# Self attention and FFN of a perceiver layer: lists of steps with distances in place of alternating generators

## The chip, the cores and the metric

The kernel runs on one core of a Trainium2 chip, in float32 with bfloat16 in the feed-forward part. The metric is the device time of the whole program in microseconds, the median of repeated runs.

## The reference

One perceiver layer on 64 batch rows. `x` has 64 rows of 64 tokens of 256 features, the context 64 rows of 256 tokens. Three sublayers follow each other, each with a residual:

```python
x = x + xattn(layernorm(x), ctx, ctx)   # 16 heads of 16; 64 queries on 256 keys of the same batch row
x = x + attn(layernorm(x))              # causal self attention, 16 heads of 16, 64 tokens
x = x + ffn(layernorm(x))               # gate, up: 256 -> 1024; down: 1024 -> 256

def _act_quant(x):                      # each row of activations to 8-bit whole numbers
    scale = 127.0 / clip(max(abs(x), axis=-1), 1e-05)
    return clip(round(x * scale), -128, 127) / scale
# weights: to -1, 0, 1 times the mean of their absolute values
gate = silu(bitlinear(x, w_gate)); up = bitlinear(x, w_up)
return bitlinear(gate * up, w_down)
```

## The kernel before

**Tiling.** The 64 batch rows form 8 groups of 8 (G = 8). A group has 512 tokens, 4 tiles of 128 (NI = 4). `x` of a group is one tile of 128 x 4 x 256 with 4 buffers (`load_x`, L79). The context comes for two batch rows at a time (`load_ctx`, L84, 2 buffers). PSUM holds one tile of four banks for cross attention's scores (`ps_sc`, L66) and four tiles of one bank for everything else (`mm_tile`, L69). A new `mm_tile` waits until the last reader of the tile that had its bank is done.

**The order of the work** is written out by hand: from L630 on, the program order of each engine (TensorE, ScalarE, VectorE, GpSimd) is the order in which the Python code issues. An engine works through its queue in that order.

**The main loop** (L644) has one iteration for each batch row n; I call it a *place*, and count the places 1 to 8 of a group of eight (n % 8 = 0 is place 1). A place does cross attention for its row:

- `max_rows` (L271): TensorE transposes the row maxima (`mtp`, L273), ScalarE copies them (`mT`, L275);
- `probabilities` (L278): scores transposed (`scT`, L286 and L293), exp on ScalarE (`PT`, L299), sums of two halves on GpSimd (`PS`, L301);
- `project` (L617): a quarter of the keys or values of the next pair of rows, twice (`k_a`, L209; `v_a`, L229), copied by ScalarE (L222, L232);
- `scores_max` (L250) for the next row: scores (`sc`, L258), their maxima on VectorE (`nm`, L262), and four small VectorE operations that split them into three bfloat16 parts (L265 to L268), which the next `mtp` reads;
- `cross_av` (L305): products with the values and sums (`av`, L313, L318), and ScalarE's `keep` (L322). The rest, `cross_out` (L325: three VectorE operations that read `av` and write `yT_a`), is done in the next place, after `mtp` is issued.

**Filler work.** While group g does cross attention, the self attention of group g-1 and the FFN of group g-2 are done in between. `prepare` (L594) normalises the next group's x and makes its queries, one `yield` in each place. Self attention (`self_attention`, L332) and FFN (`ffn`, L482) are Python generators. `fill` (L578) is called six times in each place (48 times in a group): it takes one step, up to the next `yield`, from one of the two generators, in turn. Self attention has 24 steps, the FFN 19, so both are through before a group ends; `drain` (L586) takes what is left at the start of the next group.

What a step gives to VectorE is in the step itself, with two exceptions, which go into a list `later` and are issued at the start of the next `fill`: the product of `silu` and `up` (`hidden`, L522) and `keep` of self attention (L420).

Steps of self attention that matter here: `add_projected` (L234: two tiles of output projection `o_a` or `o_s` for one VectorE add of 128 x 512 at L242), `ln_stats` (L167), `ln_rstd` (L173, seven GpSimd operations), `ln_apply` (L187), `transposed` (`tp_s`), queries and keys, `scores` (`ssc`, L366; VectorE adds the mask and takes maxima, L372, L375; GpSimd subtracts, L376), `exps` (L380), `normalise` (VectorE sums and reciprocals, L386, L387; GpSimd multiplies, L388), `transpose` (`stp`, L396, copied at L401), `product` (`sav`, L411, L417).

Of the FFN: `ln_rstd`, `ln_apply`, `row_scale` (L469) and the rounding (L495, L498), the transposes `qtp` (L504, copied at L506); then for tile i the two halves of `gate_up` (L510; `silu`, L517), `scale_hidden` (L526: absolute maxima and small operations on VectorE, then ScalarE's scaling, L529), `round_hidden` (L531), `turn_hidden` (`hqtp`, L538, copied at L540), `down` (L542) and its add (L547). The result is stored by a DMA on GpSimd's queue (L565).

**The tail** (L683 to L689). After the last row, self attention 7 and FFN 6 alternate without cross attention, then FFN 7 runs alone.

Of the kernel before, what the change touches and what calls it, by code (L numbers as in the profile page):

```python
# [55 lines left out]
def tile_perceiver(ctx: ExitStack, tc: tile.TileContext, a: dict, out: bass.AP):  # L57
# [39 lines left out]
    bqc, bqkc = constant("bq_c"), constant("bqk_c")  # L97
    sel = constant("sel", BF16)
# [28 lines left out]
    def out_bias(w, vcol, brow, name):  # L127

        rep = small.tile([P, KC, P], F32, tag="rep", name=f"rep_{name}", bufs=1)
# [57 lines left out]
    def ln_apply(src, mv, y, name):  # L187

        xn = act.tile([P, NI, D], F32, tag="xn", name=f"xn_{name}", bufs=3)
        for i in range(NI):  # L190
            nc.vector.tensor_scalar(xn[:, i, :], src[:, i, :], mv[:, i, 0:1], y[:, i:i + 1],
                                    ALU.subtract, ALU.mult)
        return xn
# [40 lines left out]
    def add_projected(w, yT, xg, name, i0):  # L234

        pm = mm_tile(f"o_{name}_{i0}")
        for i in range(2):
            for kc in range(KC):
                nc.tensor.matmul(pm[:, i * D:(i + 1) * D],  # L239
                                 yT[:, kc, (i0 + i) * P:(i0 + i + 1) * P], w[:, kc, :],  # L240
                                 start=(kc == 0), stop=(kc == KC - 1))
        nc.vector.tensor_tensor(xg[:, i0:i0 + 2, :], pm.rearrange("p (i d) -> p i d", d=D),  # L242
                                xg[:, i0:i0 + 2, :], ALU.add)
# [61 lines left out]
    def cross_av(n, pT, pS, v):  # L305
# [17 lines left out]
        return a4, t  # L323
# [7 lines left out]

    def self_attention(g, xg, yTa):  # L332
        nm = f"s{g}"
        mv = moments(nm)
        for i0 in range(0, NI, 2):
            add_projected(wT["o"], yTa, xg, f"a{g}", i0)
            ln_stats(xg, nm, mv, (i0, i0 + 1))
            yield
        y = ln_rstd(mv, nm)
        yield  # L340
        xn = ln_apply(xg, mv, y, nm)
        yield
        xnT = act.tile([P, KC, NT], F32, tag="xnT", name=f"xnT_{nm}")
        for kc in range(KC):
            transposed(xn, nm, xnT, kc)
        yield
        qm = act.tile([P, KC, G, 2, T], F32, tag="sqm", name=f"sqm_{g}", bufs=1)
        kT = act.tile([P, KC, NT], F32, tag="skT", name=f"skT_{g}", bufs=1)
        v = act.tile([P, NI, D], F32, tag="sv", name=f"sv_{g}", bufs=1)
        for hg in range(KC):  # L350
            queries(wqkv, bqm2, xnT, nm, qm, hg)
            yield
            keys(wqkv, D, bqkc[:, KC + hg:KC + hg + 1], xnT, nm, kT, hg)
            yield
        yT = act.tile([P, KC, NT], F32, tag="yT", name=f"yT_{nm}", bufs=3)
        s, pTs = {}, {}

        def scores(hg, j0):
# [3 lines left out]
            for b in range(G):  # L362
                for h in range(2):
                    for i in range(2):
                        r = slice(2 * E * (j0 + i), 2 * E * (j0 + i + 1))
                        nc.tensor.matmul(scs[i][h * T:(h + 1) * T, b * T:(b + 1) * T],  # L366
                                         qm[r, hg, b, h, :], kT[r, hg, b * T:(b + 1) * T],
                                         start=True, stop=True)
            for i in range(2):
                k = f"{nm}_{hg}_{j0 + i}"  # L370
                t = s[hg, j0 + i] = att.tile([P, G, T], F32, tag="s", name=f"s_{k}", bufs=4)
                nc.vector.tensor_tensor(t, scs[i].rearrange("p (b k) -> p b k", k=T),  # L372
                                        causal.unsqueeze(1).to_broadcast([P, G, T]), ALU.add)
                mx = small.tile([P, G], F32, tag="smax", name=f"smax_{k}")
                nc.vector.tensor_reduce(mx, t, AX.X, ALU.max)  # L375
                nc.gpsimd.tensor_tensor(t, t, mx.unsqueeze(2).to_broadcast([P, G, T]), ALU.subtract)  # L376
# [5 lines left out]
        def normalise(hg, j0):  # L382
            for j in (j0, j0 + 1):
                t = s[hg, j]
# [97 lines left out]
    def ffn(g, xg):  # L482
# [67 lines left out]
        for i in range(NI + 3):  # L550
            if i < NI:
                gate_up(i, 0)
            if 0 < i <= NI:
                scale_hidden(i - 1)
# [201 lines left out]
```

## Time and profile before

| | us |
|---|---|
| runs, median of 3 (1131.37 to 1132.72) | 1131.42 |
| the profiled execution | 1134.02 |
| its span, first to last instruction | 1132.3 |
| start, up to the first place of group 1 | 130.4 |
| group 1 (no FFN yet) | 111.4 |
| group 2 | 128.5 |
| groups 3 to 6, each | 129.6 to 129.7 |
| group 7, its first seven places | 116.2 |
| from the last place to the end | 127.1 |

The stretches are taken from the start times of `mtp`, one in each place. In the page, PE is TensorE's matmuls, PEld its weight loads, DVE VectorE, ACT ScalarE, POOL GpSimd; a float32 matmul stands there as two. PEclk is the granted clock of TensorE in tenths, in 40 slices of the span. A row of a window table gives a stretch in us from the span's start, its length, then busy us (and instructions) of PE, PEld, DVE, ACT and POOL, TensorE's granted clock, the DMA share and GB/s. A row of waits gives who waited, for whom, the us in total, how often, and the longest. A row of groups gives line, engine, operation, tiles out<-in, shapes and count, then busy us, mean ns of one, idle us before them and what ended it.

### The profile page before, as it was taken

The numbers are of one execution on the slowest core, as the hardware profiler recorded it, in microseconds if no ns is written. First come the engines' busy times: TensorE is split into PE (matmuls) and PEld (weight loads), VectorE is DVE, ScalarE is ACT, GpSimd is POOL, SyncE is SP. The second block draws the span as 40 slices with busy tenths as digits, with TensorE's granted clock in tenths as the row PEclk, the third lists the DMA queues.
The fourth block names the chain that finished last, engine by engine and source line by source line (L and its number), as shares of the span: only waits on it lengthen the run. The fifth ranks groups of instructions, "written<-read, shape, count | busy, mean of one in ns | idle before, by whom it ended". The sixth has DMA issues, their size and how long they took to land.

```text
span 1132.3 us, 28299 instructions
## 1 busy us (share of the span) xinstructions
PE 955.4 (84%) x12366; PEld 645.5 (57%) x12366; DVE 785.4 (69%) x1560; ACT 591.9 (52%) x862; POOL 405.1 (36%) x452
## 2 busy tenths in 40 slices
PE   6987888988899898998898898998989988977655
PEld 3554556665576556665575555765566655754533
DVE  2566757566787867777777867867777756877745
ACT  2423354436764377535764367644775357626624
POOL 0344436232255313542254413451336312541520
PEclk9978998999999898998989998998989988998857
DMA  6111000100001000010001000010001000000000
GB/s 219 58 57 57 20 20 3 39 20 20 20 2 58 20 20 20 21 57 20 20 2 58 20 20 20 20 58 20 2 20 39 20 20 1 3 21 1 1 19 19
DMA packets 10059, 32.65 MB, mean 29 GB/s; under 512 B 2128, under 2 KB 2640, under 8 KB 9552
## 3 DMA queue, kind: packets, MB, share of 16 engines
q1 hardware_dynamic: 7056, 26.22, 6.5%
q0 software_dynamic: 1152, 4.19, 0.9%
q8 instruction: 97, 1.59, 0.6%
q10 hardware_dynamic: 1728, 0.43, 0.2%
q14 instruction: 26, 0.21, 0.1%
HBM read 26.65 MB, written 4.19 MB: 27 GB/s over the span
## 4 chain that ended last, share of the span: by engine, by line
PE 51%; DVE 21%; ACT 10%; issue 6%; POOL 2%; POOLq 0%; ACTq 0%; DVEq 0%
PE k_a L209 6%; PE sc L258 5%; PE av L313 4%; PE v_a L229 4%; PE scT L293 4%; ACT PT L299 3%; DVE nm L262 3%; PE ssc L366 3%; PE down_f L545 3%; PE o_s L239 3%; PE q_s L209 2%; PE stp L396 2%; PE v_s L229 2%; PE q_a L209 2%; PE av L318 2%
## 5 line engine op out<-in xcount | busy, mean ns | idle before, releaser
L301 POOL TENSOR_TENSOR PS<-PT 128x512 f32<-128x512 f32 x128 | 160.3, 1273 | 363.4 <-ACT PT L299 363.4
L262 DVE TENSOR_REDUCE nm<-sc 128x8 f32<-128x2048 f32 x64 | 146.6, 2290 | 142.1 <-PE sc L258 142.1
L299 ACT ACTIVATE PT<-scT 128x1024 f32<-128x1024 f32 x128 | 124.0, 1021 | 86.4 <-PE scT L293 79.9
L209 PE MATMUL k_a<-cT,wk 128*128 128x512 f32 x256 | 125.2, 613 | 8.8 <-DMA wk<-in_wk_dram 5.5
L229 PE MATMUL v_a<-wv,cT 128*128 128x256 f32 x512 | 129.4, 397 | 2.3 <-ACT qm L217 2.2
L376 POOL TENSOR_TENSOR s_s<-s_s,smax_s 128x512 f32<-128x512 f32 x64 | 66.7, 1047 | 158.0 <-DVE smax_s L375 154.5
L229 PEld LDWEIGHTS v_a<-wv,cT 128*128 128x128 f32 x512 | 96.1, 196 | 22.3 <-issue 4.6
L322 ACT ACTIVATE keep<-av,par 128x256 f32<-128x256 f32 x64 | 30.3, 473 | 118.4 <-PE av L318 99.6
L258 PE MATMUL sc<-kT,qm 32*128 32x256 f32 x1024 | 78.7, 423 | 14.3 <-ACT PT L299 12.3
L523 DVE SCALAR_TENSOR_TENSOR h_f<-up_f,units,silu_f 128x512 f32<-128x512 f32 x64 | 47.7, 746 | 58.6 <-ACT silu_f L517 32.8
L388 POOL TENSOR_TENSOR s_s<-s_s,stot_s 128x512 f32<-128x512 f32 x64 | 68.9, 1098 | 39.3 <-ACT spT L401 30.1
L293 PE MATMUL scT<-qm,kT 32*128 32x128 f32 x2048 | 81.5, 285 | 0.0
L209 PEld LDWEIGHTS k_a<-cT,wk 128*128 128x128 f32 x256 | 47.5, 195 | 52.3 <-issue 40.6
L313 PE MATMUL av<-PT,v 128*32 128x128 f32 x2048 | 74.7, 289 | 1.7 <-ACT PT L299 1.7
L293 PEld LDWEIGHTS scT<-qm,kT 32*128 32x128 f32 x2048 | 74.7, 201 | 0.4
L258 PEld LDWEIGHTS sc<-kT,qm 32*128 32x128 f32 x1024 | 48.7, 194 | 45.5 <-ACT PT L299 25.5
L222 ACT ACTIVATE kT<-k_a,bk_c 128x512 f32<-128x512 f32 x64 | 44.3, 691 | 53.8 <-PE k_a L209 53.3
L313 PEld LDWEIGHTS av<-PT,v 128*32 128x32 f32 x2048 | 55.6, 115 | 25.5 <-issue 20.5
L372 DVE TENSOR_TENSOR s_s<-ssc,causal 128x512 f32<-128x512 f32 x64 | 43.9, 685 | 29.2 <-PE ssc L366 28.5
L327 DVE RECIPROCAL keep<-keep 128x128 f32<-128x128 f32 x64 | 61.0, 953 | 2.2
L366 PE MATMUL ssc<-skT,sqm 32*64 32x64 f32 x2048 | 45.4, 240 | 17.5 <-ACT silu_f L517 11.9
L232 ACT COPY v<-v_a 128x512 f32<-128x512 f32 x64 | 37.5, 587 | 43.1 <-PE v_a L229 43.1
(153 smaller groups left out, 1885.8 us busy)
## 6 DMA issues: line engine op xcount, KB each, us to landing
cT<-in_ctx_dram SPq DMA_DIRECT2D x32, 512.0 KB, 3.3
x<-in_x_dram SPq DMA_DIRECT2D x8, 512.0 KB, 3.5
out_dram<-x POOLq DMA_DIRECT2D x8, 512.0 KB, 3.0
wffn_gate<-in_wgate_dram SPq DMA_DIRECT2D x1, 1024.0 KB, 6.0
wffn_up<-in_wup_dram SPq DMA_DIRECT2D x1, 1024.0 KB, 5.4
wffn_down<-in_wdown_dram SPq DMA_DIRECT2D x1, 1024.0 KB, 5.4
wqkv<-in_wqkv_dram SPq DMA_DIRECT2D x1, 768.0 KB, 6.1
wk<-in_wk_dram SPq DMA_DIRECT2D x1, 256.0 KB, 4.2
```

The costliest lines, as they stand in the source:

```text
L209: nc.tensor.matmul(pm, w[:, kc, c0:c0 + P], src[:, kc, :], start=(kc == 0), stop=(kc == KC - 1))
L229: nc.tensor.matmul(pm[:, i * D:(i + 1) * D], src[:, kc, (i0 + i) * P:(i0 + i + 1) * P], w[:, kc, c0:c0 + D], start=(kc == 0), stop=(kc == ...
L258: nc.tensor.matmul(sc[:, j, hg * S:(hg + 1) * S], qm[r, hg, b, :, :].rearrange("p h q -> p (h q)"), kT[r, hg, k0:k0 + S], start=True, stop ...
L262: nc.vector.tensor_reduce(nm, sc.rearrange("p j (c s) -> p j c s", s=S), AX.X, ALU.max, negate=True)
L293: nc.tensor.matmul(sc[:, j, o:o + P], kT[r, hg, k0 + c * P:k0 + (c + 1) * P], qm[r, hg, b, :, :].rearrange("p h q -> p (h q)"), start=Fals ...
L299: nc.scalar.activation(pT[:, j:j + 2].rearrange("p j c k n -> p j (c k n)"), sc[:, j:j + 2, :], AF.Exp)
L301: nc.gpsimd.tensor_tensor(pS[:, j:j + 2], pT[:, j:j + 2, :, 0, :], pT[:, j:j + 2, :, 1, :], ALU.add)
L313: nc.tensor.matmul(av[2 * E * j:2 * E * (j + 1), hg * P:(hg + 1) * P], v[:, (n % 2) * SC + c, d0:d0 + 2 * E], pT[:, j, hg, c, :], start=(c ...
L327: nc.vector.reciprocal(t[:, KC:, :], t[:, KC:, :])
L366: nc.tensor.matmul(scs[i][h * T:(h + 1) * T, b * T:(b + 1) * T], qm[r, hg, b, h, :], kT[r, hg, b * T:(b + 1) * T], start=True, stop=True)
L376: nc.gpsimd.tensor_tensor(t, t, mx.unsqueeze(2).to_broadcast([P, G, T]), ALU.subtract)
L388: nc.gpsimd.tensor_tensor(t, t, tot.unsqueeze(2).to_broadcast([P, G, T]), ALU.mult)
```

## The change

Self attention and FFN become lists of steps. A step is a triple: whether it gives TensorE work, a distance, and a function. A step may run only when that many places of the order (calls of `fill`) have passed since the step before it. Both lists together have 40 steps with TensorE work (26 and 14), and `fill` is called five times in each place, 40 times in a group.

```diff
-    streams = [iter(()), iter(())]
+    LEFT = 4
+    streams = [[], []]
+    count = [1, 1]
+    ready = [0, 0]
+    place = [0]
     later = []
-    turn = [0]
+    owner = [None]
 
-    def flush():
-        while later:
-            later.pop(0)()
-
-    def fill(k=1):
-        for _ in range(k):
-            flush()
-            for _ in range(2):
-                turn[0] = 1 - turn[0]
-                if next(streams[turn[0]], 0) is None:
-                    break
+    def flush(us=1e9):
+        while later and us > 0:
+            t, f = later.pop(0)
+            us -= t
+            f()
+
+    def run(k):
+        if any(o == k for o in owner[1:]):
+            flush()
+            del owner[1:]
+        _, _, f = streams[k].pop(0)
+        had = len(later)
+        f()
+        if len(later) > had:
+            owner.append(k)
+        if streams[k]:
+            ready[k] = place[0] + streams[k][0][1]
+
+    def fill():
+        place[0] += 1
+        able = [k for k in range(2) if len(streams[k]) > LEFT * k and ready[k] <= place[0]]
+        for k in list(able):
+            if not streams[k][0][0]:
+                run(k)
+                if not streams[k] or ready[k] > place[0] or not streams[k][0][0]:
+                    able.remove(k)
+        if able:
+            run(max(able, key=lambda k: (not k and len(streams[0]) > count[0] - NI,
+                                         len(streams[k]) / count[k] - 0.25 * k)))
```

`LEFT = 4`: the last four steps of an FFN wait in the list until the next FFN's steps are appended (`begin`), so they run in the next group, ahead of that FFN's head. `finish(0)` takes the place of `drain` for self attention; the FFN isn't drained.

The main loop (`cross_out` is now in `later` too, put there by `cross_av`):

```diff
         mT = max_rows(n, ms)
-        if kept is not None:
-            cross_out(n - 1, *kept, yTs[(n - 1) // G])
+        flush()
         if b == 0 and g:
-            drain(0)
-            drain(1)
-            streams[:] = [self_attention(g - 1, xs[g - 1], yTs[g - 1]),
-                          ffn(g - 2, xs[g - 2]) if g > 1 else iter(())]
+            finish(0)
+            begin(0, self_attention(g - 1, xs[g - 1], yTs[g - 1]))
+            if g > 1:
+                begin(1, ffn(g - 2, xs[g - 2]))
         fill()
+        if b == 2:
+            next(ahead, None)
+        flush()
         pT, pS = probabilities(n, qms[g], kTs[bp], mT)
         fill()
+        flush()
         if bp + 1 < B // 2:
             project(bp + 1, 2 * (n % 2))
         fill()
+        flush()
         if n + 1 < B:
             ms = scores_max(n + 1, qms[(n + 1) // G], kTs[(n + 1) // 2])
-        kept = cross_av(n, pT, pS, vs[bp])
+        cross_av(n, pT, pS, vs[bp], yTs[g])
         next(ahead, None)
         fill()
         if bp + 1 < B // 2:
             project(bp + 1, 2 * (n % 2) + 1)
-        fill(2)
-        if b == 0 and g + 1 < NG:
+        fill()
+        if b == 1 and g + 1 < NG:
+            if g > 2:
+                while len(streams[1]) > count[1]:
+                    run(1)
             if g:
                 xs[g + 1] = load_x(g + 1)
             ahead = prepare(g + 1)
```

The lists of steps:

```diff
+        return [
+            *(step(True, 1, (add_cross, i)) for i in range(NI)), step(False, 1, (root,)),
+            step(False, 2, (norm,)), step(True, 1, (turn, 0)), step(True, 1, (turn, 1)),
+            step(True, 1, (query, 0)),
+            step(True, 1, (key, 0)), step(True, 1, (query, 1)), step(True, 1, (key, 1)),
+            step(True, 1, (scores, 0, 0)), step(True, 1, (value, 0)), step(True, 1, (scores, 0, 2)),
+            step(True, 1, (value, 2), (exps, 0, 0)), step(False, 1, (normalise, 0, 0), (exps, 0, 2)),
+            step(True, 2, (transpose, 0, 0), (normalise, 0, 2)), step(True, 1, (scores, 1, 0)),
+            step(True, 1, (transpose, 0, 2)), step(True, 1, (scores, 1, 2)),
+            step(True, 1, (product, 0), (exps, 1, 0)), step(False, 1, (normalise, 1, 0), (exps, 1, 2)),
+            step(True, 2, (transpose, 1, 0), (normalise, 1, 2)), step(False, 1, (add_bias, xg, bo2_r, 0)),
+            step(True, 1, (transpose, 1, 2)), step(True, 1, (product, 1), (add_bias, xg, bo2_r, 2)),
+            *(step(True, 1, (add_self, i)) for i in range(NI))]
...
+        def first_half(i):
+            if i >= 2 and i - 2 < NI:
+                round_hidden(i - 2)
+            if i < NI:
+                gate_up(i, 0)
+            if i >= 3:
+                down(i - 3)
+        def second_half(i):
+            if i < NI:
+                gate_up(i, 512)
+            if 0 < i <= NI:
+                later.append((2.1, lambda: scale_hidden(i - 1)))
+            if i >= 2:
+                turn_hidden(i - 2)
...
+        steps = [(False, 1, root), (False, 2, norm), (False, 1, row_scales), (False, 2, round_rows),
+                 (True, 1, turn_rows)]
+        for i in range(NI + 3):
+            steps.append((True, 1, lambda i=i: first_half(i)))
+            if i < NI + 2:
+                steps.append((True, 1, lambda i=i: second_half(i)))
+        return steps + [(False, 1, store)]
```

The VectorE part of most steps goes into `later`: masked scores and maxima with GpSimd's subtraction, the division, the adds of the projections with their statistics, the FFN's row scales and rounding products, the `silu` product, `scale_hidden`, the subtraction of `round_hidden`, the add of `down`. ScalarE's scaling of the hidden rows moves from `scale_hidden` to `round_hidden`, a step later.

Smaller edits: `add_projected` does one tile of 256 columns instead of two; the line that loads the constants `bq_c` and `bqk_c` stands twice; `rep` takes a buffer of the tag `PS` instead of its own; `xn` has 2 buffers instead of 3; `prepare` issues its statistics in one step, through `later`, and its queries a `yield` later; x of the next group is loaded in place 2 instead of 1, after what is left of the FFN before has run.

The tail:

```diff
-    drain(0)
-    drain(1)
-    streams[:] = [self_attention(NG - 1, xs[NG - 1], yTs[NG - 1]), ffn(NG - 2, xs[NG - 2])]
-    fill(60)
-    streams[:] = [ffn(NG - 1, xs[NG - 1]), iter(())]
-    fill(60)
+    finish(0)
+    begin(0, self_attention(NG - 1, xs[NG - 1], yTs[NG - 1]))
+    begin(1, ffn(NG - 2, xs[NG - 2]))
+    while streams[0]:
+        fill()
+        flush()
+    begin(1, ffn(NG - 1, xs[NG - 1]))
+    finish(1)
```

## The prediction

> **What bounds the kernel now.** I read the page's busy shares and slices first, then the busy times of each engine in the eight places (places 1 to 8: one batch row each, from one transpose of the row maxima, L273, to the next) of one steady group, then TensorE's waits in that group, then the rows by form, and last the two stretches after the last place.
>
> ```profile
> PE 955.4 (84%) x12366; PEld 645.5 (57%) x12366; DVE 785.4 (69%) x1560; ACT 591.9 (52%) x862; POOL 405.1 (36%) x452
> PEclk9978998999999898998989998998989988998857
> ```
>
> TensorE is the busiest, but 84% is a mean over unlike stretches, and the clock row has dents. One group, place by place (columns: length, busy times, granted clock):
>
> ```profile
> 629.60:641.50 11.90, 11.15 (x131) 7.72 (x130) 8.93 (x21) 3.85 (x6) 2.49 (x2) 1.00 0.13 45
> 641.50:660.70 19.20, 14.75 (x147) 10.37 (x146) 12.85 (x31) 8.38 (x12) 4.59 (x8) 0.82 0.09 28
> 660.70:677.00 16.30, 15.73 (x138) 7.90 (x138) 11.41 (x25) 12.75 (x17) 4.54 (x8) 1.00 0.01 2
> 677.00:698.20 21.20, 16.67 (x287) 12.66 (x286) 14.47 (x31) 17.21 (x21) 4.49 (x4) 0.96 0.08 26
> 698.20:716.30 18.10, 17.75 (x232) 11.94 (x231) 15.33 (x31) 11.69 (x17) 9.08 (x8) 0.86 0.00 1
> 716.30:731.30 15.00, 14.20 (x281) 10.67 (x277) 11.90 (x18) 8.21 (x13) 7.29 (x7) 1.00 0.01 4
> 731.30:749.60 18.30, 15.65 (x219) 10.00 (x214) 12.93 (x20) 9.93 (x18) 11.42 (x11) 1.00 0.24 88
> 749.60:759.30 9.70, 9.56 (x131) 7.42 (x129) 8.17 (x19) 3.21 (x5) 4.58 (x8) 1.00 0.01 2
> sum 129.70, PE 115.46 PEld 78.68 DVE 96.00 ACT 75.24 POOL 48.49; mean PE 14.43 PEld 9.84 DVE 12.00 ACT 9.40 POOL 6.06
> ```
>
> A group takes 129.7 us: TensorE is busy 115.5 and idle 14.2. The filler work is uneven: the first and last place hold little, the fourth is full (ScalarE 17.2 us). The idle time lies in the second, fourth and seventh place; VectorE's 96 us is not far below TensorE. TensorE's own waits there:
>
> ```profile
> PE qtp_f L504 <- DVE q_f L498: 3.6, 1, 3.6
> PE sc L258 <- ACT PT L299: 1.6, 1, 1.6
> PE scT L286 <- ACT mT L275: 1.6, 2, 0.9
> PE ssc L366 <- ACT silu_f L517: 1.4, 1, 1.4
> PE down_f L545 <- DVE keep L326: 1.2, 1, 1.2
> ```
>
> The largest is the FFN's head; the others are queues of ScalarE and VectorE, or a PSUM bank not yet read.
>
> **What the skill says.** "TensorE: Matmul & The Clock Gate", What's actually happening: the array drops to half clock after about 3.4 us without activity. The trace agrees: the 3.6 us wait is followed by one 6.8 us stretch at half clock, the 1.0 and 1.4 us waits in the fourth place by another, so less than a whole idle window is enough here. Same page, Architectural detail (the array as sub-arrays): VectorE and ScalarE are strictly first in, first out; the trace shows the same (an ssc wait on silu whose matmul had long ended). "ScalarE: Activation LUTs", What ACT_TABLE_LOAD costs: 1283 ns, which is the trace's number; the drain it adds does not show here, silu starts within 0.03 us.
>
> ```profile
> L262 DVE TENSOR_REDUCE nm<-sc 128x8 f32<-128x2048 f32 x64 | 146.6, 2290 | 142.1 <-PE sc L258 142.1
> L299 ACT ACTIVATE PT<-scT 128x1024 f32<-128x1024 f32 x128 | 124.0, 1021 | 86.4 <-PE scT L293 79.9 <-issue 6.3
> L517 ACT ACT_TABLE_LOAD x27 | 34.6, 1283 | 0.5
> ```
>
> **The change part by part.** The built orders of both kernels give what stands in each place; durations are those of the trace before, at full clock from the first matmul of a step to the first of the next: a place's fixed part 7.63 us (mtp 0.2, scT 1.2, sc 1.1, av 1.45, two projections 1.83 each), ssc pair 1.16, stp pair 0.93, sav pair 1.09, q/k/v 1.83, gate+up 0.96, down 0.97, o_a and o_s 0.92 to 0.98 per tile, hqtp 0.54.
>
> *TensorE work* is unchanged: 8 x 7.63 + 48.8 of steps = 109.9 us a group. So 115.5 busy holds 5.6 us of half clock, and 129.7 - 109.9 = 19.8 us is the most a steady group can give. After the change the places hold 12.3, 11.9, 16.1, 13.1, 13.7, 14.9, 15.9 and 12.1 us: evener.
>
> *Removed.* The FFN's head (norm, scale, round) now stands one to two places ahead of qtp, so 3.6 us and its half clock go in the steady groups. A step always stands between mtp and scT: the 1.6 us on mT goes.
>
> *Added or moved to VectorE's queue.* Nearly everything a step sends to VectorE is now put off and queued behind the next flush. What comes behind a place's maxima is therefore late by: nm and its four small operations 3.1 us from the end of sc, cross_out 1.8 (0.47, 0.95, 0.29 and gaps), and xn of the next queries 1.4 where it falls. The stalls left, one by one (need against TensorE's cover after sc):
> - place 2, hqtp of the last tile: 3.1 + 1.8 + add and statistics 1.1 + hq 0.7 = 6.7 against 5.4: 1.4 us (with the hop).
> - places 3/4, the second score pair needs the first pair's banks: 3.1 + 1.8 + q 0.7 + 3 x 0.7 = 7.7 against 6.5: 1.2. Second gate half needs av's bank: 3.1 + 1.4 + 0.5 = 5.0 against 4.2: 0.8.
> - place 5, stp needs the division: 3.1 + 1.4 + 1.8 + sum and reciprocal 0.85 + GpSimd 1.05 = 8.2 against 6.2: 2.0; its second tile 0.6; silu behind a table load at the end 0.5.
> - place 6: ScalarE has 17.0 us of work against 14.9. silu of the third tile comes at about 12.0 (kT 0.7, mT 0.3, silu 0.7, table 1.28, PT 2.04, skeep 0.94, exps 1.25, v 0.6, exps 1.25, h 1.23, table 1.28, silu 0.7). The product with up waits for it on VectorE, and nm of the next row stands behind: 12.7 + 3.1 + 0.5 = 16.3 before av's bank is read and v_a can go. Its 1.84, stp 0.93 and hops end the place at 19.2: 4.3 us.
> - place 7: stp and sav wait for exps and copies, 1.7. Place 8: mT stands behind table, silu and hqT, 1.5. Place 1: o_a behind cross_out, 0.5.
>
> Sum 14.5 us. As most pieces are under 2.2 us I count half a half-clock stretch a group, 3.4 x 0.5 = 1.7 (bounds 0 and 6). Group: 109.9 + 14.5 + 1.7 = 126.1, 3.6 less than 129.7. The walk ignores what I cannot see: one us of error in each place either way.
>
> *Split adds* (L242): four of 256 columns for two of 512. No row of before is exactly this; the nearest, the 256-wide down add, is 0.48 against 0.69, so 4 x (0.96 - 0.69) = 1.1 us of VectorE a group; hidden where it has slack, 1.1 where not. I take it as within the sums above.
> *Loads.* load_x moves one place later, on SP behind load_ctx, and behind the FFN's store on GpSimd's queue. Store 3.0, load 3.5 alone, perhaps 6 beside the context load: the statistics of x, first on VectorE in place 3, may wait 0 to 4 us, but 2.3 us of statistics and 4.0 of scaling have 9.8 us before nm. I take 0; cost 0 to 1 a group. Two constants are loaded twice on ScalarE's queue before sel: 0, at most 0.5, as the first place starts only at 27.8. Two xn buffers for three: the tile two back was read places before: 0. Table loads 52 for 54: -2 x 1.28 of ScalarE, nothing.
>
> *Other stretches.* Group 1 has no FFN and was 111.4 with 11.5 idle and crowded into four places; its TensorE work is 95.5. Spread, with stalls like places 2 to 5, and mT bare in two places, about 106: -5. Group 2 keeps the qtp wait (the FFN's head there begins as it did), 128.5 to 125.5: -3. Group 7's seven places: -3. The start: 0.
>
> ```profile
> 1013.00:1089.00 76.00, 54.03 (x592) 36.27 (x591) 51.72 (x119) 37.09 (x52) 24.28 (x31) 0.82 0.02 8
> 1089.00:1132.30 43.30, 20.70 (x104) 11.52 (x104) 23.14 (x56) 15.94 (x18) 2.53 (x7) 0.70 0.03 12
> ```
>
> The tail first runs self attention 7 beside FFN 6, then FFN 7 alone. Now the four projections come first and the score pairs stand 7 us sooner, so I walk the 76 us to about 63; but the FFN's last four steps are held back, and they run after self attention, ahead of FFN 7's root on GpSimd (behind the store): maxima 2.0, h 1.3, hq 0.7, hqtp 0.6, copy 1.05, down 1.05, add 0.5, store issue 0.7 = 8; FFN 7 itself +1. Net -4, bounds -12 and +8.
>
> Sum: -5 - 3 - 4 x 3.6 - 3 - 4 = -29.4. The profiled execution took 1134.0 us (span 1132.3, 1.7 around it), 2.6 above the median of the runs: 1134.0 - 29.4 = 1104.6, as a median **1102.0**. Own range 1078 to 1122.
>
> **Rivals.**
> *The distances hold* (0.18). If VectorE's queue drains ahead of my walk, only ScalarE's pinch in place 6 and some hops stay, 5 us a group at full clock: 115 for 129.7, four times -14.7; groups 1, 2 and 7 -25 together, tail -6: 1131.4 - 90 = 1042. For it: VectorE's 96 us in 115. Against: first in, first out; nm stands behind everything flushed.
> *VectorE's queue becomes the bound* (0.26; slower). In places 5 and 6 VectorE has about 14 and 15 us with gaps against TensorE's 13.7 and 14.9. If a silu or an exp comes 2 us later than I reckon, nm, maxima, mtp and scT slip together, TensorE idles over 3 us there and two half-clock stretches return. It decides from 18.1 us of stalls a group (14.5 + 3.6), counting half clock as I did; with 19 of stalls and 5 of half clock a group is 134: 5 x 4.2, and tail +5: 1157. For it: ScalarE's 17 us and in before a fourth place with the same load took 21.2. Against: the four lighter places refill.
> *The stalls only change place* (0.06): what qtp gives, hqtp and stp take: 1131.
>
> **Chances and range.** Likeliest 0.50. Anything within 0.2% (2.3 us, what a measurement can tell) is 0.04, out of the third rival and the edges. Faster 0.70 (0.50 + 0.18 + 0.02), slower 0.26. The range reaches to 1062 and 1146: it leaves out about a tenth on either side, and holds the unknown loads and tail.
>
> **What would show it.** Right: qtp's wait gone from group 3 on and lengths from 12 to 19 within a group, the sixth place the longest with gate or v_a waiting on silu and keep; stp waiting on GpSimd's division; hqtp on hq; o_s to qtp of FFN 7 with down and hqtp of FFN 6 between. Wrong: clock dents in more than every second group (second rival); TensorE idle under 6 us a group (first); x landing late in front of VectorE's statistics; a self attention 7 that is not shorter.

## The result and the profile after

| | before | after |
|---|---|---|
| median of the runs | 1131.39 us (1130.96 to 1132.72) | 1120.65 us (1120.22 to 1122.11) |
| ratio | | 0.9905, 95% interval 0.9888 to 0.9922 |
| profiled execution; its span | 1134.0; 1132.3 us | 1121.0; 1119.0 us |
| mean granted TensorE clock | 0.924 | 0.931 |

The change is 10.7 us faster. The forecast was 29.4 us. First the busy shares and the clock in forty slices of the changed kernel:

```profile
PE 939.8 (84%) x12323; PEld 641.6 (57%) x12366; DVE 777.7 (70%) x1592; ACT 589.8 (53%) x860; POOL 408.7 (37%) x452
PEclk9888999998999999999989998999989999898866
```

The shares say almost nothing: they are those of before. The clock row shows fewer dents in the middle and much the same end (8866 where 8857 was). So the stretches have to be compared one by one. A stretch runs from the first row-maxima transpose (L273) of a group to that of the next; the tail begins with the last such transpose.

| stretch | before | after | measured | forecast |
|---|---|---|---|---|
| start to group 1 | 130.4 | 133.3 | +2.9 | 0 |
| group 1 | 111.4 | 109.7 | -1.7 | -5 |
| group 2 | 128.5 | 131.9 | +3.5 | -3 |
| groups 3 to 6 | 518.7 | 502.1 | -16.6 | -14.4 |
| group 7 and tail | 243.3 | 241.9 | -1.4 | -7 |
| sum (spans) | | | -13.3 | -29.4 |

The steady groups, 3 to 6, did what was forecast. Everything else fell short, by 18 us together. (The profiled executions are 13 us apart and the medians 10.7, because the profiled execution of before lay 2.6 above its median.) Here is one steady group after the change, place by place (columns: from:to in us, length, busy times of PE, PEld, DVE, ACT and POOL with their instruction counts, granted clock, DMA share, GB/s):

```profile
624.40:636.40 12.00, 11.98 (x137) 8.25 (x137) 11.38 (x27) 4.06 (x8) 2.49 (x2) 1.00 0.09 33
636.40:650.10 13.70, 11.71 (x152) 8.95 (x151) 10.29 (x22) 7.00 (x11) 7.77 (x15) 1.00 0.21 76
650.10:665.80 15.70, 15.70 (x198) 9.23 (x197) 13.65 (x32) 8.10 (x12) 4.69 (x8) 1.00 0.12 38
665.80:680.50 14.70, 13.03 (x210) 9.96 (x209) 10.22 (x18) 9.95 (x16) 6.62 (x6) 1.00 0.05 14
680.50:700.90 20.40, 18.09 (x269) 12.37 (x268) 12.73 (x25) 10.81 (x16) 8.58 (x8) 0.75 0.05 18
700.90:720.00 19.10, 14.78 (x220) 10.15 (x218) 16.67 (x29) 14.49 (x22) 7.85 (x7) 1.00 0.01 3
720.00:736.40 16.40, 15.51 (x219) 9.78 (x218) 11.05 (x26) 11.57 (x18) 8.65 (x7) 1.00 0.09 33
736.40:750.80 14.40, 11.92 (x153) 9.54 (x151) 9.21 (x22) 9.40 (x12) 2.50 (x2) 1.00 0.05 11
sum 126.40, PE 112.71 PEld 78.23 DVE 95.20 ACT 75.39 POOL 49.16; mean PE 14.09 PEld 9.78 DVE 11.90 ACT 9.42 POOL 6.14
```

TensorE's idle time in places 2, 4 and 7, 11.6 us in the group before, is 4.6 us here, and seven of the eight places run at full clock. Place 5 is the odd one: its clock of 0.75 is one stretch of 10.2 us at half clock. The whole group is 3.3 us shorter than before; 2.8 of them are TensorE's busy time (112.7 for 115.5 us, with 10.2 for 13.7 us at half clock), and only 0.5 its idle time (13.7 for 14.2). TensorE's longest waits in the same window (line and operation, what it waited for: us in total, times, longest):

```profile
PE stp L417 <- POOL s_s L409: 3.0, 2, 2.3
PE mtp L273 <- DVE keep L326: 2.1, 2, 1.1
PE hqtp_f L551 <- DVE hq_f L546: 2.0, 1, 2.0
PE v_a L231 <- DVE keep L326: 1.9, 1, 1.9
PE o_s L240 <- ACT silu_f L532: 1.4, 1, 1.4
PE up_f L527 <- DVE yT_s L445: 1.1, 1, 1.1
PE ssc L381 <- DVE s_s L390: 0.9, 1, 0.9
PE gate_f L527 <- DVE keep L326: 0.8, 1, 0.8
```

The wait of the FFN's transpose (L519 now), 3.6 us before, is gone. What stands here instead are the stalls that the prediction had listed. The window is a hair longer than the group, so the 1.1 us ahead of a row-maxima transpose is in it twice.

Group 2, which has the same code but no FFN that runs on into it, reads otherwise:

```profile
PE up_f L527 <- ACT silu_f L532: 4.5, 1, 4.5
PE qtp_f L519 <- DVE q_f L512: 4.0, 1, 4.0
PE stp L417 <- DVE keep L326: 2.4, 1, 2.4
PE up_f L527 <- DVE s_s L390: 1.5, 1, 1.5
```

It keeps the wait at the head, as forecast (4.0 us; 3.6 before), and gets a new one of 4.5 us on silu in its sixth place. Each goes with 6.8 us at half clock. At the start VectorE reads (start, duration, operation, and in brackets the idle time before and what ended it):

```profile
9.57 0.43 DVE L172 BATCH_NORM_STATS2 st_a<-x 128x6 f32<-128x256 f32 x1 [3.61 <-DMA x<-in_x_dram]
12.79 0.36 DVE L124 TENSOR_SCALAR bqm<-qpar,bq_c 128x2 f32<-128x2 f32 x2 [2.79 <-DMA bq_c<-in_bq_c_dram]
13.05 0.17 DVE L173 BATCH_NORM_AGGREGATE mv_a<-st_a 128x2 f32<-128x6 f32 x1
```

VectorE waits 2.8 us for the second copy of a 1 KB constant, with most of the statistics and the first normalisation behind it. Last, the tail, counted from the last row-maxima transpose: until self attention 7's statistics, and from there on.

```profile
983.80:1064.60 80.80, 61.78 (x709) 42.17 (x714) 59.52 (x144) 42.84 (x58) 27.46 (x33) 0.85 0.02 8
1064.60:1119.00 54.40, 23.93 (x124) 12.95 (x122) 26.27 (x66) 17.31 (x19) 3.36 (x8) 0.65 0.05 20
```

The first line was to fall by 13 us, from 83.6 before to about 71 us, and is 80.8. The second line is 11 us longer than the 43.3 of before: FFN 6's last steps come first.

### The profile page after: what moved, and what is told of

Read it like the earlier page. It is cut to its first block, busy times and chain, and to the rows that moved or that the text cites. A ratio compares the mean times of both kernels' runs of the same rounds, so it can differ in the third digit from the quotient of the medians.

```text
span 1119.0 us, 28320 instructions
## 1 busy us (share of the span) xinstructions
PE 939.8 (84%) x12323; PEld 641.6 (57%) x12366; DVE 777.7 (70%) x1592; ACT 589.8 (53%) x860; POOL 408.7 (37%) x452
## 4 chain that ended last, share of the span: by engine, by line
PE 40%; DVE 27%; ACT 13%; issue 7%; POOL 3%; POOLq 0%; ACTq 0%; DVEq 0%
DVE nm L262 7%; PE k_a L211 5%; PE v_a L231 4%; PE sc L258 4%; PE scT L293 4%; ACT PT L299 3%; DVE keep L327 3%; PE q_s L211 3%; PE k_s L211 2%; PE ssc L381 2%; PE av L313 2%; PE stp L417 2%; POOL s_s L409 2%; ACT h_f L541 2%; ACT L532 2%
## 5 line engine op out<-in xcount | busy, mean ns | idle before, releaser
L211 PE MATMUL k_a<-cT,wk 128*128 128x512 f32 x256 | 130.2, 634 | 5.9 <-DMA wk<-in_wk_dram 5.7
L231 PEld LDWEIGHTS v_a<-wv,cT 128*128 128x128 f32 x512 | 99.0, 201 | 28.9 <-DVE keep L326 9.7
L322 ACT ACTIVATE keep<-av,par 128x256 f32<-128x256 f32 x64 | 30.3, 473 | 127.1 <-PE av L318 127.1
L258 PE MATMUL sc<-kT,qm 32*128 32x256 f32 x1024 | 75.9, 411 | 2.4 <-ACT PT L299 1.3
L211 PEld LDWEIGHTS k_a<-cT,wk 128*128 128x128 f32 x256 | 48.4, 200 | 49.1 <-issue 39.1
L313 PE MATMUL av<-PT,v 128*32 128x128 f32 x2048 | 71.6, 281 | 1.1 <-ACT PT L299 1.1
L313 PEld LDWEIGHTS av<-PT,v 128*32 128x32 f32 x2048 | 53.5, 112 | 23.9 <-issue 15.9
L417 PE MATMUL stp<-ident,s_s 128*128 128x128 f32 x256 | 43.6, 315 | 24.2 <-POOL s_s L409 17.8
```

Of the source, the lines that this page charges most:

```text
L211: nc.tensor.matmul(pm, w[:, kc, c0:c0 + P], src[:, kc, :], start=(kc == 0), stop=(kc == KC - 1))
L231: nc.tensor.matmul(pm[:, i * D:(i + 1) * D], src[:, kc, (i0 + i) * P:(i0 + i + 1) * P], w[:, kc, c0:c0 + D], start=(kc == 0), stop=(kc == ...
L258: nc.tensor.matmul(sc[:, j, hg * S:(hg + 1) * S], qm[r, hg, b, :, :].rearrange("p h q -> p (h q)"), kT[r, hg, k0:k0 + S], start=True, stop ...
L313: nc.tensor.matmul(av[2 * E * j:2 * E * (j + 1), hg * P:(hg + 1) * P], v[:, (n % 2) * SC + c, d0:d0 + 2 * E], pT[:, j, hg, c, :], start=(c ...
L417: nc.tensor.transpose(pt[:, bp * P:(bp + 1) * P], t[:, 2 * bp:2 * bp + 2, :].rearrange("p b k -> p (b k)"), ident)
```

## The experiments

All kernels are the changed kernel with the edit shown. The changed kernel's own median is 1120.65 us; the ratios are to the kernel before, whose median in the different sets of runs lay between 1131.2 and 1133.2 us. Two us between two of these medians therefore say little.

**One load of the two constants.**

```
-    bqc, bqkc = constant("bq_c"), constant("bqk_c")
     bqc, bqkc = constant("bq_c"), constant("bqk_c")
```

> The changed kernel without the second load of the two constants. My theory: the 1 KB load of the query bias, issued a second time, lands at 12.7 us, VectorE's product with it (L124) waits for it and stands ahead of the first normalisation; so the first row-maxima transpose comes at about 28 us instead of 32.9, the stretch from the start to group 1 falls from 133.3 to about 130, and the total from 1120.6 to about 1117.5 (1115.5 to 1118.5). Rival (the second load is harmless; the start is later for another reason, such as the order of ScalarE's first table loads): first transpose stays at 32 to 33 us and the total at 1120.6.

Measured: 1115.2 us (ratio to before 0.9839, 0.9817 to 0.9860). The first row-maxima transpose comes at 27.7 instead of 32.9 us, which is 5.2 of the 5.4 us by which the median falls. VectorE at the start of this run:

```profile
6.73 0.36 DVE L123 TENSOR_SCALAR bqm<-qpar,bq_c 128x2 f32<-128x2 f32 x2 [0.98 <-DMA bq_c<-in_bq_c_dram]
7.00 0.35 DVE L123 TENSOR_SCALAR bqm<-qpar,bqk_c 128x2 f32<-128x2 f32 x2
9.14 0.43 DVE L171 BATCH_NORM_STATS2 st_a<-x 128x6 f32<-128x256 f32 x1 [1.79 <-DMA x<-in_x_dram]
```

The product with the bias is done before x has landed, and my theory holds: in the eleven traces with the second load the first place starts at 31.7 to 33.6 us, in the three without it at 27.5 to 28.1. Its size was too small. Of the 5.2 us, 3.6 are the later normalisation; the other 1.6 are the first queries' product on TensorE, which takes 5.3 us in place of 3.7: 3.4 us there are at half clock, after TensorE had been idle for 3.3. The start to group 1 showed only 2.9 us because the rest of group 0 was 100.4 us for 102.6 before; that is not shown to be a gain, for it varies between 99.8 and 102.8 us over the runs.

**The tail without the limit.**

```
+    left[0] = 0
     while streams[0]:
```

> The changed kernel, but after the last place the FFN's last four steps are no longer held back, so that FFN 6 ends beside self attention 7. My theory: FFN 7's root no longer stands 9.4 us behind the statistics but about 2; self attention 7 itself is the same or up to 2 us longer; total 1113 to 1115. Rival (ScalarE and VectorE bound the tail: whatever FFN 6 does there lengthens self attention 7 by as much): total 1119 to 1122, the statistics end 6 to 8 us later.

Measured: 1122.21 us (0.9902, 0.9880 to 0.9924). (Here and below, `left[0]` is `LEFT` made changeable; it starts at 4.) This tells nothing on the tail: the order of instructions is that of the changed kernel. In the tail the list with the larger share left always goes first, and FFN 6 still had five steps when self attention 7 ended, so the limit never decided. It stands as a repeat, and shows the scatter: 1.6 us.

**The next queries' norm behind the division.**

```
-        next(ahead, None)
+        if b != 3:
+            next(ahead, None)
         fill()
...
+        if b == 3:
+            flush()
+            next(ahead, None)
```

> The changed kernel, but the normalisation of the next queries (four VectorE operations, 1.37 us together) is issued at the end of place 4, behind the division of the first scores instead of ahead of it. My theory: the wait of the first self-attention transpose for GpSimd's division in place 5 falls from 2.26 us to about 0.9, and the 10.2 us at half clock that begin with it go: a steady group from 126.3 to about 121.5, total 1100 to 1106. Rival A (the wait shrinks, the half clock stays, as shorter waits are enough to set it off): 1.4 a group, total about 1114. Rival B (the norm only stands in front of something else, mT or the next transposes): 1118 to 1122.

Measured: 1109.34 us (0.9788, 0.9765 to 0.9810), halfway between my theory and its rival A. Places 5 and 6 of the same group, and TensorE's longest waits in it:

```profile
674.10:689.60 15.50, 13.91 (x270) 9.56 (x270) 13.03 (x26) 10.78 (x16) 8.60 (x8) 1.00 0.07 29
689.60:710.40 20.80, 16.48 (x218) 11.30 (x219) 18.27 (x35) 14.63 (x22) 7.85 (x7) 0.92 0.01 2
```

```profile
PE hqtp_f L551 <- DVE hq_f L546: 2.0, 1, 2.0
PE v_a L231 <- DVE keep L326: 1.9, 1, 1.9
PE stp L417 <- POOL s_s L409: 1.5, 2, 1.2
PE o_s L240 <- ACT silu_f L532: 1.4, 1, 1.4
```

Four VectorE operations of 1.37 us together were the cause of 5 us in place 5: the wait on the division falls from 2.3 to 1.2, and the 10.2 us at half clock go. But they are now in place 6, whose VectorE is the fullest (16.7 to 18.3 us busy): it is 1.7 us longer, with 3.4 us at half clock. Groups 4 to 6 are 122.8 for 126.3. The clock is confirmed as the larger part of this stall. That it can be removed at no cost elsewhere is not.

**Nothing put off.**

```
         f()
-        if len(later) > had:
-            owner.append(k)
+        flush()
```

> The changed kernel with the same lists and distances, but what a step sends to VectorE is issued with the step and no longer put off behind the next scores. Theory 1 (the order of the lists is what gains; putting off serves only the row maxima): row maxima wait behind the work of the steps, TensorE idles for the maxima in the full places; a steady group 128 to 132 instead of 126.3, total 1127 to 1150. Theory 2 (putting off is what makes the stalls: everything stands behind maxima and cross_out): the waits on hq, the division and silu shrink and the total falls to 1100 to 1115.

Measured: 1121.87 us (0.9899, 0.9878 to 0.9920): neither, and it is a test of neither. Groups 3 to 6 are the same to 0.1 us, because the orders of instructions nearly are: between the point where a step's VectorE part is put off and the flush, almost nothing else enters VectorE's queue. In groups 1 and 2 its order is the same; in groups 3 to 7 one rounding (`q_f`) comes three operations sooner. What stands behind the maxima stands there by the place of the step in the list.

**The FFN not run on.**

```
             finish(0)
+            finish(1)
             begin(0, self_attention(g - 1, ...
```

> The changed kernel, but the FFN's remaining steps are run at the start of each group (as before the change), and the next FFN begins there. My theory: the run-on is what puts the FFN's head one to two places ahead of its transpose; without it groups 3 to 6 get the wait of qtp on q back (4 us and a stretch of 6.8 us at half clock), as group 2 has it in the changed kernel: each about 132 to 134 instead of 126.3 (123.1 in group 3), total 1140 to 1155. Rival (the distances, not the run-on, make room for the head): groups stay at 126 to 128 and the total at 1118 to 1128.

Measured: 1204.55 us (1.0640, 1.0624 to 1.0656), about three times as bad as expected and 73 us slower than before. Groups 3 to 6 are 141 to 143 us. TensorE's longest waits in group 5:

```profile
PE up_f L527 <- ACT silu_f L532: 4.5, 1, 4.5
PE qtp_f L519 <- DVE q_f L512: 4.0, 1, 4.0
PE hqtp_f L551 <- DVE hq_f L546: 3.9, 1, 3.9
PE stp L417 <- DVE keep L326: 2.4, 1, 2.4
```

Three of these four are group 2's, to the tenth: a group whose FFN begins with it gets the head's 4.0 us and silu's 4.5 us. The fourth is the hidden rows' transpose among the steps that now run by themselves at the group's start. Against the changed kernel the group is idle 9.6 us more, and has 23.9 for 10.2 us at half clock. So the run-on carries the steady groups: 15 to 20 us each. The run does not separate the head from the bare steps.

**All distances one.**

```
-            step(False, 2, (norm,)), ...
+            step(False, 1, (norm,)), ...
...
-            step(True, 2, (transpose, 0, 0), ...
+            step(True, 1, (transpose, 0, 0), ...
```

and the same for the second transpose and the FFN's norm and rounding.

> The changed kernel with all distances of two set to one: the norm of self attention and of the FFN directly after its root, the rounding directly after the scaling, the transposes of the probabilities directly after the division. Theory 1 (the distances carry the gain): VectorE's norm waits for GpSimd's root, TensorE for the division; groups 3 to 6 from 126.3 to 130 to 136, total 1135 to 1165. Theory 2 (what counts is the run-on of the FFN and the evenness of the list; VectorE's queue is late anyway): groups at 125 to 128, total 1116 to 1126.

Measured: 1130.8 us (0.9973, 0.9962 to 0.9984), between the totals of the two theories. Group 1 is 116.1 instead of 109.7 us and group 6 130.3 instead of 126.3. Groups 4 and 5 are 126.0, nearly as with the distances, but by another sum. TensorE waits 4.1 and 2.2 us there for the division, instead of 2.3 and 0.8: so far theory 1 is right. In exchange the waits of 1.9 us (`v_a`), 1.4 (`o_s`) and 0.8 (`gate`) are gone, and 6.8 instead of 10.2 us run at half clock. Groups 5 and 6 of this run:

```profile
633.50:759.50 126.00, 111.65 (x1538) 76.81 (x1545) 94.19 (x197) 75.53 (x110) 49.37 (x55) 0.97 0.08 27
759.50:889.80 130.30, 115.84 (x1537) 80.40 (x1544) 93.39 (x196) 75.43 (x110) 49.15 (x55) 0.93 0.08 26
```

The order of instructions is the same in both and the waits nearly so, yet TensorE is busy 4.2 us longer in the second, with 17.1 for 6.8 us at half clock. Group 1 has 17.1 us at half clock where the changed kernel has 3.4. So most of the 8 to 10 us that this run loses are half clock, and how much of it a group gets does not follow from its order of instructions alone. What the distances are worth in a steady group stays open.

**The first FFN later.**

```
                 begin(1, ffn(g - 2, xs[g - 2]))
+                if g == 2:
+                    ready[1] += 9
```

> The changed kernel, but the first FFN (group 2, where no earlier FFN runs on) is begun nine fills later, so that its head stands beside scT of the third place and its transpose in the fourth, as in groups 3 to 6. My theory: the wait of qtp (4.0 us) and the half clock behind it go and group 2 falls from 131.9 to 126 to 128, total 1115 to 1117. Rival (the steps behind it only move into group 3 or the idle time comes back in places 4 to 6): group 2 and 3 together 253 to 256 as now (255.0), total 1119 to 1122.

Measured: 1117.16 us (0.9877, 0.9861 to 0.9894). Group 2 is 125.0 for 131.9 and group 3 126.4 for 123.1, so that half of the gain is given back. The rival's reason for that does not hold: group 3 has the same steps in the same places and the same waits of 0.8 and 2.3 us ahead of the first `stp` as before this edit, but 10.2 instead of 3.4 us at half clock behind them. TensorE's longest waits in group 2 are now mostly a steady group's, and those on q and on silu in the sixth place are gone:

```profile
PE stp L417 <- POOL s_s L409: 3.0, 2, 2.3
PE tp_s L204 <- DVE xn_s L193: 2.4, 2, 1.5
PE v_a L231 <- DVE keep L326: 1.9, 1, 1.9
PE o_s L240 <- ACT silu_f L532: 1.4, 1, 1.4
```

**The hidden rows scaled on GpSimd.**

```
-            nc.scalar.activation(h[i], h[i], AF.Identity, scale=scs[i], bias=magic)
+            nc.gpsimd.tensor_scalar(h[i][:, 0, :], h[i][:, 0, :], scs[i], MAGIC, ALU.mult, ALU.add)
```

> The changed kernel with the scaling of the hidden rows (L541, 1.23 us on ScalarE) on GpSimd, as one multiply and add by a column of scales and a constant. Theory 1 (place 6 is long because ScalarE has more work there than TensorE): place 6 from 19.1 to 17 to 18, the wait on silu at the self output projection falls, a group 1 to 2 us shorter, total 1110 to 1116. Theory 2 (VectorE's queue sets place 6: 16.7 us busy of 19.1): 0 to 1 a group, total 1117 to 1122. If GpSimd needs over 2 us for it and hq waits, hqtp comes later and the total is 1122 to 1130.

Measured: 1177.19 us (1.0405, 1.0389 to 1.0421), worse than any theory had it, and not because GpSimd is slow at it (1.12 us, ScalarE 1.24). Groups 4 to 6 are 136.5 us. In place 2 the operation stands behind the root of self attention in GpSimd's queue, which waits for statistics of its own (columns as in VectorE's listing of the start):

```profile
660.85 0.24 POOL L178 TENSOR_SCALAR var_s<-mv_s 128x4 f32<-128x4 f32 x1 [7.58 <-DVE mv_s L173]
661.17 1.04 POOL L180 TENSOR_TENSOR rstd_s<-var_s,mhalf 128x4 f32<-128x4 f32 x1
...
663.32 1.12 POOL L541 TENSOR_SCALAR h_f<-h_f,qscale_hf 128x1024 f32<-128x1024 f32 x1
664.48 0.69 DVE L546 TENSOR_SCALAR hq_f<-h_f 128x1024 bf16<-128x1024 f32 x1 [3.72 <-POOL h_f L541]
```

The transpose of the hidden rows waits 5.8 us there instead of 2.0, with 6.8 us at half clock. Later in the group TensorE waits 2.7 us for another such transpose and 3.0 us ahead of a projection, and 20.5 instead of 10.2 us of the group are at half clock; what brings these later waits was not followed up. Whether ScalarE or VectorE sets place 6 is left open by this run.

**FFN 7 beside the end of FFN 6.**

```
-    begin(1, ffn(NG - 1, xs[NG - 1]))
-    finish(1)
+    begin(0, ffn(NG - 1, xs[NG - 1]))
+    left[0] = 0
+    while streams[0] or streams[1]:
+        fill()
+        flush()
```

> The changed kernel, but in the tail FFN 7 is begun beside the last steps of FFN 6 and no longer behind them: its root, norm and scaling are issued as soon as the last statistics are, the end of FFN 6 runs in between. (The earlier run with the tail's own limit at zero had the same order of instructions as the changed kernel and tested nothing.) My theory: the last steps of FFN 6 stand 9.4 us ahead of the root now; the root comes 1 to 3 us behind the statistics, the end of FFN 6 costs 1 to 3 us in FFN 7's head: total 1113 to 1117. Rival (VectorE and ScalarE are shared, so FFN 7's head is later by what FFN 6's end takes of them): total 1118 to 1122.

Measured: 1112.77 us (0.9836, 0.9821 to 0.9850). Counted from the last row-maxima transpose, the statistics end at 81.2 us (80.8), FFN 7's root begins at 81.3 instead of 90.2, and the tail is 128.2 for 135.2. The theory holds.

**Self attention 7 alone.** Here FFN 6 begins when self attention 7 has ended; only FFN 5's last steps stand beside it. The total, 1138.2 us in one run, is no comparison.

```
+    left[0] = 19
     while streams[0]:
         fill()
         flush()
+    left[0] = 0
```

> The changed kernel, but in the tail no step of FFN 6 runs beside self attention 7; FFN 6 and then FFN 7 follow it alone. The total is longer by most of an FFN and is not the point; the point is when, counted from the last row-maxima transpose, the last statistics of self attention 7 end (80.8 us in the changed kernel, 83.7 in the kernel before). My theory (self attention 7 shares VectorE and ScalarE with FFN 6, which costs it 12 to 20 us): 60 to 68 us, and the forecast of 13 us for it was out of reach only because FFN 6 stands in the same queues. Rival (its own chain of scores, maxima, exponentials, division and transposes is that long, and FFN 6 fills gaps): 74 to 80 us, and no order of FFN 6 could have brought the 13 us. Total 1145 to 1165.

Measured: the first product (L434) starts at 49.1 us (52.3 beside FFN 6, 62.4 before the change), the statistics end at 67.5 (80.8). FFN 6 costs self attention 7 13.3 us, ten of them in its second half. Which shared engine costs the most was not separated.

**FFN 6 held back in that half.** On top of FFN 7's early begin, FFN 6 stops ahead of its third tile until the second divisions are issued:

```
     while streams[0]:
+        left[0] = 10 if len(streams[0]) > 7 else 0
         fill()
...
-    begin(0, ffn(NG - 1, xs[NG - 1]))
+    last = ffn(NG - 1, xs[NG - 1])
+    begin(0, last[:4])
...
+    begin(1, last[4:])
+    finish(1)
```

> The tail as in the run with FFN 7 begun beside the end of FFN 6 (1112.8), and besides FFN 6's third tile onward is held back until the second half of self attention 7 has its exponentials and divisions issued. My theory: the ten us that self attention 7 has gained by its first product are lost because the second half's exponentials and divisions stand behind FFN 6's maxima and scaling on VectorE and ScalarE; held back, the last statistics come 4 to 7 us sooner, FFN 6's end then takes 1 to 3 back: tail from 128.2 to 123 to 126, total 1107 to 1111. Rival (the work held back comes later one for one, as nothing else fills the tail): tail 128 to 131, total 1112 to 1116.

Measured: 1116.29 us (0.9843, 0.9823 to 0.9863), tail 128.4, statistics end at 82.0: the rival. (The ratio is that of the run with FFN 7's early begin; the 3.5 us between the two medians do not lie in the tail.) The second transposes start 2.8 us sooner (59.7 for 62.5), but the second products at the same 69.1 us, behind what was let go.

**Four edits together**: one load, the late norm, the late first FFN, FFN 7 beside FFN 6.

> Four of the edits together: one load of the two constants, the next queries' norm behind the division in place 4, the first FFN begun nine fills later, FFN 7 begun beside the end of FFN 6. If each acts in its own stretch and they only add: 4.7 + 11.3 + 3.5 + 7.4 = 27 below 1120.6, that is 1093 to 1096 (the late head moves group 3 to the steady length, where the late norm is worth 3.5 and not 0.6: up to 3 more). Rival (the edits meet in the same places and share one gain): 1099 to 1106.

Measured: 1090.37 us (0.9618, 0.9597 to 0.9639), 30.3 below the changed kernel, the most of any kernel here. The four edits' gains, each by itself, add up to 28.1, so they do not share one gain. Groups 2 to 6 are all 122.8 to 122.9, the tail 128.0.

**The same, FFN 6 held back to the end of self attention 7** (`left[0] = 10` throughout that loop, and the end as in the held run).

> The four edits together (1090.4), and FFN 6's third tile onward is held back until self attention 7 has ended; its end then runs beside FFN 7's head. Theory A (the work shared in the tail comes back one for one, wherever it stands: VectorE and ScalarE have to do it in the end): last statistics 6 to 9 us sooner, FFN 7's transpose not sooner by as much, total 1088 to 1093. Theory B (the earlier hold brought nothing only because it was released before the second transposes): statistics at 68 to 72 us from the last row-maxima transpose, total 1082 to 1086.

Measured: 1094.65 us (0.9657, 0.9635 to 0.9680). The statistics end at 72.2 instead of 80.9, but FFN 7's transpose starts at 95.7 instead of 90.8, so that the tail is 132.2 for 128.0. By the total that is theory A, and more than one for one. Its reason, the work of VectorE and ScalarE, is not shown: FFN 7's rounding ends at 88.0, sooner than with the four edits alone (90.7). The transpose behind it is late because this edit puts FFN 7's steps from there on behind all of FFN 6's, and TensorE's last product of FFN 6 starts at 94.0. Group 2, which the edit does not touch, is 3.1 us longer in this trace, with 10.2 for 3.4 us at half clock.

## Why the prediction was wrong

*The steady groups: right, though the closeness is in part luck.* Forecast 126.1, measured 126.3. The forecast had 3.9 us less half clock and 0.3 us more idle time than before; measured are 2.8 less and 0.5 less. The stalls one by one, with the forecast in brackets: ahead of the row-maxima transpose of place 1 1.1 (0.5), hqtp in place 2 2.0 (1.4), the score pair 0.9 (1.2), the gate 0.8 (0.8), stp in place 5 2.3 (2.0, and 0.6 for a second tile that does not wait), place 6 4.3 idle (4.3), place 7 0.8 (1.7), o_s in place 8 1.4 (1.5). Most of these waits are those that the walk named, at about their sizes. But in place 6 only 1.9 of the 4.3 us are v_a's, and ScalarE's 17.0 us of work there are 14.5, so that this sum is right by luck. The longest place is the fifth (20.4 us), not the sixth, for the half clock is not half a stretch of 6.8 us but one of 10.2 us in place 5. Group 3, which has the same steps and waits, has 3.4 us of it and is 123.1. "Nearly everything a step sends to VectorE is now put off" is true, but the putting off changes nothing (the run with nothing put off).

*"Group 2 keeps the qtp wait ... -3": failed, 6.5 us of the miss.* I let it share the gain of a spread list and left its head as it was. But its FFN begins with the group: the transpose at its head stands in the second place, in a steady group in the fourth, and in the sixth place it is still a step ahead. There silu stands behind other work of ScalarE, which runs without a gap from 325.5 to 334.1 us, and TensorE waits 4.5 us for it, with another stretch at half clock. Begun later, group 2 is 125.0, 3.5 below before; 3.3 us come back in group 3, as half clock.

*"Two constants are loaded twice on ScalarE's queue before sel: 0, at most 0.5": failed, 2.9 us in the table and 5.4 us by the run with one load.* I asked when the first place starts, not what stands behind the waiting instruction: VectorE's product with the bias is ahead of the first normalisation, and that is on the path. (In the trace the second loads are issued behind that of `sel`, not before it.)

*"Now the four projections come first ... so I walk the 76 us to about 63": failed, by 10 us.* Counted from the last row-maxima transpose the 63 us mean an end of the statistics at about 71; it is 80.8. The tail had a gain of 10 us until the first product (52.3 for 62.4) and lost seven again by the statistics. The walk names no cost of FFN 6 beside self attention 7. Without FFN 6, self attention 7 ends at 67.5, so the forecast left about 3 us for it; it costs 13.3. The other two terms were near: FFN 6's steps ahead of the root 9.4 for 8, FFN 7 +1.5 for +1. Where the group ends moved too: 5.4 us of TensorE's busy time, an output tile and FFN 5's end, went from group 7 into the tail, so that -9.4 in group 7 and +8.1 in the tail are read as one.

*"Group 1 ... about 106: -5": too much, by 3.3 us.* The loads that I had left open show no cost: no wait on x stands among TensorE's in the steady groups. Group 1's trace shows three waits on mT, 3.7 us together, 2.4 on the norm, 2.0 on the division, and 1.3 of a v_a behind cross_out's PSUM bank. No run here took them apart, so the cause stays open.

*The rivals.* "The distances hold" put 5 us of stalls into a steady group; it has 13.7 idle. "VectorE's queue becomes the bound" decides from 18.1 us of stalls; they stayed below. Without the run-on the steady groups do pass that point (23.3 us idle in group 5) and go to 141 and more, with 4.5 us on silu in the sixth place as that rival had it, but also with two waits of about 4 us that it had not.

## What to carry over

When a list of steps is moved, walk the edges (the first group, the group in which a second list starts, the tail) with the same care as the steady loop; here the steady groups came out 2 us better than forecast in all, and the edges, forecast at -15 us together, came out at +3. Price a wait by what stands behind it in its in-order queue: 1 KB loaded again cost 5 us, and an operation moved to an idler engine that is not slower at it cost 56. Holding work back on a shared engine only helps if its place later is not in front of something that the end waits for. And before a difference of a few us between two groups is put down to an edit, compare their time at half clock: the same order of instructions had 6.8 us of it in one group and 17.1 in another.

## What was not expected of the hardware

In all fifteen traces the stretches at half clock begin on one grid: their starts lie whole multiples of 3.413 us apart, to within 4 ns. All but the last, which the end of the program cuts, are whole multiples of it long. In groups 1 to 7 that is 3.4, 6.8 or 10.2 us, in the tail up to 23.9. The Trainium skill, "TensorE: Matmul & The Clock Gate", What's actually happening, speaks of 3.4 us without activity. Here shorter waits are enough, and the length of a wait does not tell its cost. In the changed kernel a wait of 0.77 us and, 1.1 us later, one of 2.26 go with 10.2 us at half clock in groups 4 to 6, but with 3.4 in group 3. One of 1.99 in place 2 has none there, but 3.4 us in group 6 of the run with all distances one. With 1.2 us in place of the 2.26 there is none in groups 4 to 6 of the late norm, but 3.4 us in group 7 of the changed kernel. Which share of a window has to be idle stays open.

The steady groups are whole multiples of the same 3.413 us, to within 0.1 us: 129.7 before (38), 126.3 after (37), 122.8 with the late norm (36), 136.5 with the scaling on GpSimd (40). They then meet the grid in the same place each time. So the late norm, which took about 1.6 us of TensorE's idle time out of a group, made it shorter by one whole step, 3.5 us. And that the forecast of 126.1 met 126.3 to 0.2 us is luck in so far as the neighbouring steps were 122.8 and 129.7. The runs without the run-on and with all distances one do not fall in step. Why the others do is not shown by a run.
